# Key sums of two softmaxes, added over partitions by transfers and VectorE in place of products with ones

## The chip, the cores and the metric

One core of a Trainium2 chip runs the whole kernel. The metric is device time in microseconds, the median of several executions of the same program; lower is better.

## The reference

The input is a batch of 8 images of 512 channels and 32x32 pixels, so 8 elements of 512 channels by 1024 tokens. Two attention layers run one after the other, all in float32. The first has a layer norm, 8 heads of 64 channels and a residual; the second has a group norm, one head of 512 channels and a residual. Cut to what matters here:

```python
# layer 0: 8 heads
scores = jnp.einsum('bqhd,bkhd->bhqk', q, k) * scale
attn = jax.nn.softmax(scores, axis=-1)
out = jnp.einsum('bhqk,bkhd->bqhd', attn, v).reshape(B, S, C)
# layer 1: one head over all channels
logits = jnp.einsum('bcn,bcm->bnm', q, k) * scale
attn = jax.nn.softmax(logits, axis=-1)
o = jnp.einsum('bnm,bcm->bcn', attn, v)
```

Each softmax needs, for every query, the sum of the exponentials over all 1024 keys. How that sum is finished is what changes.

## The kernel before

**Layout.** Scores are computed transposed: keys lie on the partitions (8 blocks of 128 keys), queries along the row. A tile of exponentials `p` is 128 keys by 1024 numbers. The sum over keys is therefore made in two parts: VectorE adds the 8 tiles `p` into one tile `sum` of 128x1024, and then the 128 partitions of that tile must be added up.

**Layer 0, by pairs.** A `Pair` is two heads with one half (512) of the queries, so an element has 8 pairs. `Pair.scores` does, for each of 8 key blocks, two matmuls (L683), one exp on ScalarE (L686) and one add on VectorE (L690, L692). `Pair.values` does 16 matmuls (L701) into a bank `acc`. The loop over pairs runs scores of pair i+1, then values of pair i. After the values of each even pair, `invert_pairs` finishes the sums of that pair and the next: four matmuls with a matrix of ones (L715), each into 32 partitions of a PSUM bank `den`, give the sums, copied over 32 partitions. Then VectorE transposes in blocks of 32 (`compact`, L491) so that 128x16 different numbers stand in one column of each block, takes reciprocals and notes a check (`invert_sums`, L657, L661); ScalarE copies rows of them to the partitions where they are used (`rr`, L728); VectorE spreads them again by transposing a broadcast (`expand`, L496). The even pair's output is copied out of `acc` by ScalarE unscaled (L705) and multiplied later (L736); the odd pair's is multiplied on the way out (L708).

**Layer 1, `Whole`.** Its products use a seven-step scheme (`STEPS`), each step a few matmuls, with copies by ScalarE (`u1`, `u2`, `u3`) and adds by VectorE (L343) between them. `key_sums` adds the exponentials into two tiles `total`, `inverse` finishes them with four matmuls (L830) and the same transposing, and `values` uses the result `rden` when a block of the output is done (L870). The product `vm` (`project_v`, two units of seven steps) lies between the scores and the values; before, `inverse` stands between its two units.

**Order.** TensorE, ScalarE, VectorE and GpSimd run their instructions in the order in which the program writes them. Small work is put into a queue `side` by `later`; `tick` takes one item from it after each key block of `values` and after each step of the seven-step products. A list `at_scores` holds work that is done after the fifth block (m = 4) of the next `scores`. Loads and stores go through SyncE's queue (SP). GpSimd's queue carries only `save_w` (L210) for the first element and then stands empty. SBUF is shared out in 46 `big` tiles of 128x1024 and 9 `half` tiles of 128x512; an instruction that writes a new tile waits until the former user of its place is done.

Of the kernel before, what the change touches and what calls it, by code (L numbers as in the profile page):

```python
# [11 lines left out]
F32 = mybir.dt.float32  # L12
I32 = mybir.dt.int32
AF = mybir.ActivationFunctionType
ALU = mybir.AluOpType
# [4 lines left out]
P = 128  # L20
# [46 lines left out]
def fast_path(ctx: ExitStack, tc: tile.TileContext, x: bass.AP, vecs: dict, weights: dict, out: bass.AP,  # L67
# [35 lines left out]
    def half_tile(name):  # L103
        return half.tile([P, HB], F32, tag="h", name=name)
# [4 lines left out]
    def bank(name):  # L109
        return ps_a.tile([P, HB], F32, tag="a", name=name)  # L110
# [201 lines left out]
    def later(*work):  # L312
        side.extend(work)
# [341 lines left out]
    def invert_sums(r, sums):  # L655

        nc.vector.reciprocal(r, sums)  # L657
        i = n_checks[0]
        n_checks[0] += 1
        rows = sums.shape[0]  # L660
        nc.vector.scalar_tensor_tensor(sums, sums, 1.0, r, ALU.mult, ALU.add, accum_out=checks[:rows, i : i + 1])  # L661


    class Pair:
# [29 lines left out]
                    while at_scores:  # L694
                        at_scores.pop()()

        def values(self):
            acc = bank(f"acc_{self.tag}")
            for m in range(NM):
                for i in range(2):  # L700
                    nc.tensor.matmul(acc[i * D : (i + 1) * D, :], value_of(self.vt, m, self.c * P + i * D, D),  # L701
                                     self.p[m][:, ts(i, HB)], start=(m == 0), stop=(m == NM - 1))
                tick()
            if self.c % 2 == 0:
                nc.scalar.copy(self.o, acc)  # L705
            else:
                until(lambda: self.rden is not None)
                nc.vector.tensor_mul(self.o, acc, self.rden)  # L708

    def invert_pairs(two):  # L710


        den = bank(f"den_{two[0].tag}")
        for k in range(4):
            nc.tensor.matmul(den[ts(k, BL), :], ones[:, :BL], two[k // 2].sum[:, ts(k % 2, HB)],  # L715
                             start=True, stop=True)
        t = half_tile(f"dent_{two[0].tag}")
        r = small.tile([P, HB // BL], F32, tag="r", name=f"r_{two[0].tag}")
        rr = [small.tile([P, HB // BL], F32, tag=f"rr{n}", name=f"rr_{pair.tag}") for n, pair in enumerate(two)]
        rden = [half_tile(f"rden_{pair.tag}") for pair in two]  # L720

        def invert():
            invert_sums(r, compact(t, den))

        def copies():
            for n in range(2):
                for j in range(4):
                    nc.scalar.copy(rr[n][ts(j, BL), :], r[ts(2 * n + j // 2, BL), :])  # L728

        def rows(n):  # L730
            expand(rden[n], rr[n])
            two[n].rden = rden[n]

        at_scores.append(invert)
        later(lambda: [at_scores.pop()() for _ in list(at_scores)], copies, lambda: rows(1), lambda: rows(0),
              lambda: nc.vector.tensor_mul(two[0].o, two[0].o, rden[0]))  # L736

    def project_out(b, w, ot, stats):

# [22 lines left out]
    class Whole:  # L762
# [50 lines left out]
        def operands(self, g):  # L813
# [7 lines left out]
            for n, l, r in (("T1", "12", "11"), ("T2", "22", "T1"), ("T3", "22", "12"), ("T4", "21", "T2")):  # L821
                later(lambda n=n, l=l, r=r: sub(n, l, r))

        def inverse(self):
            b = self.b
            den = bank(f"den1_{b}")
            for a in range(2):
                for hf in range(NH):
                    k = 2 * a + hf
                    nc.tensor.matmul(den[ts(k, BL), :], ones[:, :BL], self.total[hf][:, ts(a, HB)],  # L830
                                     start=True, stop=True)
            t = half_tile(f"den1t_{b}")
            both, r = (small.tile([P, HB // BL], F32, tag=n, name=f"{n}_{b}") for n in ("both", "r1"))
            rr = small.tile([P, NH, HB // BL], F32, tag="rr", name=f"rr1_{b}")

            def invert():
                d = compact(t, den)
                nc.vector.tensor_copy(both[:D, :], d[D:, :])
                nc.vector.tensor_add(both[:D, :], both[:D, :], d[:D, :])
                invert_sums(r[:D, :], both[:D, :])  # L840

            def copies():
                for j in range(4):
                    for hf in range(NH):
                        nc.scalar.copy(rr[ts(j, BL), hf, :], r[ts(hf, BL), :])  # L845

            def rows():
                self.rden = big_tile(f"rden1_{b}")
                expand(self.rden, rr.rearrange("p a k -> p (a k)"))

            later(nothing, invert, copies, rows)

        def values(self, v):
            b = self.b
# [44 lines left out]
    with tc.manual_schedule(engines=ORDERED):  # L899
# [67 lines left out]
        for b in range(B):  # L967
            more = b + 1 < B
            stats = small.tile([P, NC, NH, 6], F32, tag="stats", name=f"stats_{b}")
            ot = {"tag": f"o_{b}"}  # L970
            first = Pair(b, 0, 0, qt, kt, vts, ot)
            first.scores(range(NM))
            q_last.rest()
            pairs = [first] + [Pair(b, hf, c, qt, kt, vts, ot) for hf in range(NH) for c in range(NC) if hf + c > 0]
            for i, p in enumerate(pairs):
                if i + 1 < len(pairs):
                    pairs[i + 1].scores(range(NM))
                if i < 2 and more:
                    until(lambda: ln.done)
                    later(*(lambda j=j, a=a, i=i: ln.affine(j, i, a) for j in range(2) for a in range(2)))  # L980
                if i == 1 and more:
                    wk_next = load_w("k", b + 1)
                if i == 6:
                    wo_now = load_w("o", b)
                if i == 7 and more:
                    hb = operands(ln.result())
                    add_operands(hb)
                p.values()
                if i % 2 == 0:
                    invert_pairs(pairs[i : i + 2])  # L990
            if more:
                k_units, kn = project(f"k{b + 1}", wk_next, bias_of("bk0"), hb, True)
                k_units[0].rest()
            wa_now = load_w("a", b)
            ob = operands(ot)
            o_units, x1 = project_out(b, wo_now, ob, stats)
            o_units[0].step(1)
            add_operands(ob)
            o_units[0].step(1)
            o_units[1].step(2)  # L1000
            for u in o_units:
                u.rest()
            wm_now = load_w("m", b)

            def meanwhile(n):
                if more:
                    k_units[1].step((2, 1, 3, 1)[n])

            h1 = group_norm(b, x1, stats, meanwhile)
            x1_away = {ik: put_away(wide(t), f"x1_away_{b}_{ik[0]}{ik[1]}") for ik, t in x1.items()}  # L1010
            h1b = operands(h1)
            add_operands(h1b)
            a_units, qa = project(f"qa{b}", wa_now, lambda oc: ua[:, oc : oc + 1], h1b)
            a_units[0].step(2)
            meanwhile(3)
            if more:
                kn_away = {ik: put_away(wide(t), f"k_away_{b + 1}_{ik[0]}{ik[1]}") for ik, t in kn.items()}
            a_units[1].step(2)
            for u in a_units:
                u.rest()  # L1020
            whole = Whole(b, qa, h1b, x1_away)
            s_units = whole.scores()
            whole.query_sums()
            for u in s_units[:2]:
                u.step(2)
            for u in s_units[:2]:
                u.rest()
            whole.key_sums(0)
            whole.operands(0)
            for u in s_units[2:]:  # L1030
                u.rest()
            whole.key_sums(1)
            whole.operands(1)
            v_units, vm = project_v(f"vm{b}", wm_now, h1b)
            v_units[0].rest()
            until(lambda: whole.summed)
            whole.inverse()
            v_units[1].rest()
            if more:
                wv_next, wq_next = load_w("v", b + 1), load_w("q", b + 1)  # L1040
            o_units = whole.values(vm)
            check = iter(()) if more else all_checks()
            for u in o_units:
                u.step(2)
                next(check, None)
            for u in o_units:
                u.rest()
            until(lambda: not side)
            if more:
                kt = {ik: block(f"k{b + 1}_again_{ik[0]}{ik[1]}") for ik in kn_away}  # L1050
                for ik, d in kn_away.items():
                    nc.sync.dma_start(out=wide(kt[ik]), in_=d)
                ln, vts, qt, q_last = next_values_and_queries(b + 1, wv_next, wq_next)
# [384 lines left out]
```

## Time and profile before

| | |
|---|---|
| three runs | 2967.59, 2969.01, 2970.05 us; median 2969.01 |
| the profiled execution | span 2967.7 us, granted TensorE clock 0.998 |
| matmuls at L715 (32 groups of 8) | 34.1 us busy |
| matmuls at L830 (8 groups of 8) | mean 604 ns of one |
| DMA | 217.32 MB, mean 73 GB/s |

A group's busy time counts the time in which at least one of its matmuls runs, so groups whose matmuls overlap show less than count times mean. Each float32 matmul of the program shows as two in the profile. A row of the profile names line, engine, operation, the tile written and the tiles read, and what the engine had waited for. The whole table of groups is long; these are the ones of attention on VectorE and ScalarE:

```profile
L686 ACT ACTIVATE p<-s 128x1024 f32<-128x1024 f32 x512 | 476.1, 1051 | 173.4 <-PE s L683 173.4
L692 DVE TENSOR_TENSOR sum<-sum,p 128x1024 f32<-128x1024 f32 x384 | 470.4, 1225 | 38.9 <-DVE sum L692 0.9
...
L728 ACT COPY rr<-r 32x16 f32<-32x16 f32 x256 | 51.7, 202 | 32.4 <-DVE r L657 28.5
```

### The profile page before, as it was taken

What the parts mean: (1) busy time and instruction counts of PE and PEld (TensorE: products, weight loads), DVE (VectorE), ACT (ScalarE), POOL (GpSimd) and SP (SyncE); (2) the same over time, 40 slices, a digit from 0 to 9 for tenths busy, and PEclk for the clock granted to TensorE, in tenths of its full rate; (3) what the DMA queues carried; (4) which work ended last, traced back from release to release, by engine and by line L of the source; (5) the groups of instructions that cost most, each with busy time, mean ns of one, the idle gap of its engine ahead of it and who ended that gap; (6) DMA issues with size and microseconds to landing.
All of it is one profiled execution on the core that took longest, in us unless ns stands there. A gap on an engine that the chain in (4) does not pass through costs nothing.

```text
span 2967.7 us, 26543 instructions
## 1 busy us (share of the span) xinstructions
PE 2945.7 (99%) x10043; PEld 1378.4 (46%) x10043; DVE 1773.6 (60%) x2266; ACT 1030.9 (35%) x1617; POOL 22.1 (1%) x37
## 2 busy tenths in 40 slices
PE   8999999999999999999999999999999999999999
PEld 4534455345543455434553345533455334553344
DVE  6676456765476654765546655576555665536744
ACT  4462215612155131641216412263222632225230
POOL 2000000000000000000000000000000000000000
PEclk9999999999999999999999999999999999999999
DMA  8103130031301213012130122201231021300201
GB/s 304 44 25 128 46 124 25 32 129 40 124 25 54 106 54 110 25 59 101 54 110 25 61 99 67 97 25 61 100 101 63 25 93 67 106 29 33 99 4 55
DMA packets 84920, 217.32 MB, mean 73 GB/s; under 512 B 8704, under 2 KB 12848, under 8 KB 84784
## 3 DMA queue, kind: packets, MB, share of 16 engines
q1 hardware_dynamic: 81616, 204.51, 19.9%
q0 software_dynamic: 3072, 11.01, 1.0%
q8 instruction: 81, 1.33, 0.2%
q14 instruction: 55, 0.45, 0.0%
q10 hardware_dynamic: 96, 0.02, 0.0%
HBM read 156.26 MB, written 59.24 MB: 73 GB/s over the span
## 4 chain that ended last, share of the span: by engine, by line
PE 97%; DVE 1%; DMA 1%; issue 0%; ACT 0%; SPq 0%; DVEq 0%
PE s L683 15%; PE acc L701 15%; PE x_o L429 6%; PE x_s L421 6%; PE y_s L421 4%; PE y_o L429 4%; PE z_o L429 4%; PE z_s L421 4%; PE x_q L404 3%; PE x_k L404 3%; PE x_vm L413 3%; PE x_qa L404 3%; PE x_v L413 3%; PE x_out L404 2%; PE y_q L404 2%; PE z_qa L404 2%
## 5 line engine op out<-in xcount | busy, mean ns | idle before, releaser
L686 ACT ACTIVATE p<-s 128x1024 f32<-128x1024 f32 x512 | 476.1, 1051 | 173.4 <-PE s L683 173.4
L692 DVE TENSOR_TENSOR sum<-sum,p 128x1024 f32<-128x1024 f32 x384 | 470.4, 1225 | 38.9 <-DVE sum L692 0.9
L701 PE MATMUL acc<-p,v 128*64 128x512 f32 x2048 | 453.6, 595 | 0.0
L683 PE MATMUL s<-q,k_again 64*128 64x512 f32 x1792 | 399.8, 596 | 0.0
L701 PEld LDWEIGHTS acc<-p,v 128*64 128x64 f32 x2048 | 141.4, 137 | 305.0 <-issue 286.1
L683 PEld LDWEIGHTS s<-q,k_again 64*128 64x128 f32 x1792 | 166.6, 186 | 232.1 <-ACT p L686 103.9
L690 DVE TENSOR_TENSOR sum<-p,p 128x1024 f32<-128x1024 f32 x64 | 78.4, 1225 | 195.2 <-ACT p L686 195.2
L421 PE MATMUL x_s<-S_qa,T_gn 128*128 128x512 f32 x256 | 120.3, 592 | 0.0
L429 PE MATMUL x_o<-T_p,S_vm 128*128 128x512 f32 x256 | 115.2, 592 | 0.0
L791 ACT ACTIVATE p<-p 128x512 f32<-128x512 f32 x128 | 80.8, 631 | 73.0 <-DVE p L343 73.0
L343 DVE TENSOR_TENSOR p<-u(1, 1)_s,y_s 128x512 f32<-128x512 f32 x32 | 22.1, 689 | 132.3 <-ACT u(1, 1)_s L434 132.3
L451 ACT ACTIVATE u(0, 0)_k<-x_k,vecs 128x512 f32<-128x512 f32 x16 | 11.0, 687 | 247.9 <-PE x_k L404 247.9
L343 DVE TENSOR_TENSOR y<-u(1, 1)_o,y_o 128x512 f32<-128x512 f32 x16 | 11.0, 688 | 132.5 <-ACT u(1, 1)_o L434 132.5
L421 PEld LDWEIGHTS x_s<-S_qa,T_gn 128*128 128x128 f32 x256 | 48.6, 190 | 61.2 <-issue 61.2
L429 PEld LDWEIGHTS x_o<-T_p,S_vm 128*128 128x128 f32 x256 | 48.6, 190 | 60.7 <-issue 60.7
L705 ACT COPY o<-acc 128x512 f32<-128x512 f32 x32 | 18.8, 586 | 155.3 <-PE acc L701 155.3
L496 DVE STREAM_TRANSPOSE rden<-rr 128x512 f32<-128x512 f32 (+1 forms) x72 | 51.6, 750 | 26.4 <-ACT rr L845 13.6
L728 ACT COPY rr<-r 32x16 f32<-32x16 f32 x256 | 51.7, 202 | 32.4 <-DVE r L657 28.5
L413 PE MATMUL x_vm<-w_m,T_gn 128*128 128x256 f32 x256 | 60.5, 379 | 0.0
L343 DVE TENSOR_TENSOR qa<-u(1, 1)_qa,y_qa 128x512 f32<-128x512 f32 x16 | 11.0, 688 | 82.4 <-ACT u(1, 1)_qa L451 82.4
L421 PE MATMUL y_s<-S_qa,gn 128*128 128x512 f32 x128 | 60.2, 593 | 0.0
L421 PE MATMUL y_s<-S_qa,T_gn 128*128 128x512 f32 x128 | 60.1, 592 | 0.0
(321 smaller groups left out, 4440.7 us busy)
## 6 DMA issues: line engine op xcount, KB each, us to landing
x<-in_x_dram SPq DMA_DIRECT2D x32, 512.0 KB, 6.5
xr<-in_x_dram SPq DMA_DIRECT2D x64, 256.0 KB, 2.6
x_away<-x SPq DMA_DIRECT2D x32, 512.0 KB
x1r<-x_away SPq DMA_DIRECT2D x64, 256.0 KB, 5.1
out_dram<-y SPq DMA_DIRECT2D x64, 256.0 KB, 2.5
k_away<-k SPq DMA_DIRECT2D x28, 512.0 KB, 2.6
k_again<-k_away SPq DMA_DIRECT2D x28, 512.0 KB, 6.3
w_o<-saved_o SPq DMA_DIRECT2D x24, 512.0 KB, 4.6
```

The source lines that it names most:

```text
L404: nc.tensor.matmul(dst, a[:, k, ts(r, P)], b[:, k, :], start=(opens and k == 0), stop=(k == 1), skip_group_check=True)
L413: nc.tensor.matmul(dst[:, ts(m, CB)], b[:, k, ts(2 * r + m, P)], a[:, k, :], start=(opens and m == 0 and k == 0), stop=(k == 1), skip_grou ...
L421: nc.tensor.matmul(dst, b[:, k, ts(r, P)], a[:, k, :], start=(opens and k == 0), stop=(k == 1), skip_group_check=True)
L429: nc.tensor.matmul(dst, a[:, m, ts(r, P)], b[m // 2][:, m % 2, :], start=(opens and m == 0), stop=(m == NM // 2 - 1), skip_group_check=True)
L496: nc.vector.transpose(t.rearrange("p (k i) -> p k i", i=BL), r.unsqueeze(2).to_broadcast((P, r.shape[1], BL)))
L683: nc.tensor.matmul(s[:, ts(i, HB)], self.k[m // 4][r, ts(m % 4, P)], self.q[r, :], start=True, stop=True)
L686: nc.scalar.activation(p, s, AF.Exp, scale=1.0 / float(D) ** 0.5)
L690: nc.vector.tensor_add(self.sum, self.p[0], p)
L692: nc.vector.tensor_add(self.sum, self.sum, p)
L701: nc.tensor.matmul(acc[i * D : (i + 1) * D, :], value_of(self.vt, m, self.c * P + i * D, D), self.p[m][:, ts(i, HB)], start=(m == 0), stop ...
L728: nc.scalar.copy(rr[n][ts(j, BL), :], r[ts(2 * n + j // 2, BL), :])
L791: nc.scalar.activation(dest(i, k), dest(i, k), AF.Exp, scale=float(C) ** -0.5)
```

## The change

The partitions of the sums are added by transfers. `halve` adds the upper 64 partitions of a sum to the lower 64 with an accumulating DMA transfer issued from GpSimd. `fold` then brings each half row of 512 as 2x32 partitions into a 32-partition quarter of a half tile, the first 32 by a plain transfer and the second 32 by an accumulating one. VectorE transposes the folded tile in blocks of 32 and reduces each block's row of 32 (`folded_sums`), which gives the same 128x16 sums as `compact` did.

For the pairs, this is done for the first three groups of each element; the last group keeps the products with ones. In the folded groups the inversion moves one pair later (it is put into `at_scores` after the odd pair), both pairs' outputs are copied by ScalarE unscaled, and both are multiplied by VectorE later. For `Whole`, the four matmuls of `inverse` go; `fold` is put into `side` after the last key sums; and `inverse` moves from between the two `vm` units to after the first step of the first output unit, written directly and not through `side`.

The diff, cut:

```diff
--- before.py
+++ after.py
@@ -694,46 +694,77 @@
                     while at_scores:
                         at_scores.pop()()
-        def values(self):
+        def values(self, scaled):
             acc = bank(f"acc_{self.tag}")
             for m in range(NM):
                 for i in range(2):
                     nc.tensor.matmul(acc[i * D : (i + 1) * D, :], value_of(self.vt, m, self.c * P + i * D, D),
                                      self.p[m][:, ts(i, HB)], start=(m == 0), stop=(m == NM - 1))
                 tick()
-            if self.c % 2 == 0:
+            if not scaled:
                 nc.scalar.copy(self.o, acc)
             else:
                 until(lambda: self.rden is not None)
                 nc.vector.tensor_mul(self.o, acc, self.rden)
-    def invert_pairs(two):
-        den = bank(f"den_{two[0].tag}")
-        for k in range(4):
-            nc.tensor.matmul(den[ts(k, BL), :], ones[:, :BL], two[k // 2].sum[:, ts(k % 2, HB)],
-                             start=True, stop=True)
-        t = half_tile(f"dent_{two[0].tag}")
-        r = small.tile([P, HB // BL], F32, tag="r", name=f"r_{two[0].tag}")
-        rr = [small.tile([P, HB // BL], F32, tag=f"rr{n}", name=f"rr_{pair.tag}") for n, pair in enumerate(two)]
-        rden = [half_tile(f"rden_{pair.tag}") for pair in two]
-        def invert():
-            invert_sums(r, compact(t, den))
-        def copies():
+    def fold(f, q, t, cols):
+        for n in range(2):
+            nc.gpsimd.dma_start(out=f[ts(q, BL), :], in_=t[ts(n, BL), cols], accum_op=ALU.add if n else ALU.bypass)
+    def halve(t):
+        nc.gpsimd.dma_start(out=t[:D, :], in_=t[D:, :], accum_op=ALU.add)
+    def folded_sums(d, t, f):
+        nc.vector.transpose(t, f)
+        nc.vector.tensor_reduce(d, t.rearrange("p (k i) -> p k i", i=BL), mybir.AxisListType.X, ALU.add)
+    class PairSums:
+        def __init__(self, two):
+            self.two, self.tag = two, two[0].tag
+            self.r = small.tile([P, HB // BL], F32, tag="r", name=f"r_{self.tag}")
+            self.rr = [small.tile([P, HB // BL], F32, tag=f"rr{n}", name=f"rr_{p.tag}") for n, p in enumerate(two)]
+        def fold(self):
+            self.f = half_tile(f"fold_{self.tag}")
+            for pair in self.two:
+                halve(pair.sum)
+            for n, pair in enumerate(self.two):
+                for i in range(2):
+                    fold(self.f, 2 * n + i, pair.sum, ts(i, HB))
+        def invert_folded(self):
+            d = small.tile([P, HB // BL], F32, tag="d", name=f"d_{self.tag}")
+            folded_sums(d, half_tile(f"foldt_{self.tag}"), self.f)
+            invert_sums(self.r, d)
+        def product(self):
+            self.den = bank(f"den_{self.tag}")
+            for k in range(4):
+                nc.tensor.matmul(self.den[ts(k, BL), :], ones[:, :BL], self.two[k // 2].sum[:, ts(k % 2, HB)],
+                                 start=True, stop=True)
+        def invert(self):
+            invert_sums(self.r, compact(half_tile(f"dent_{self.tag}"), self.den))
+        def copies(self):
             for n in range(2):
                 for j in range(4):
-                    nc.scalar.copy(rr[n][ts(j, BL), :], r[ts(2 * n + j // 2, BL), :])
-        def rows(n):
-            expand(rden[n], rr[n])
-            two[n].rden = rden[n]
-        at_scores.append(invert)
-        later(lambda: [at_scores.pop()() for _ in list(at_scores)], copies, lambda: rows(1), lambda: rows(0),
-              lambda: nc.vector.tensor_mul(two[0].o, two[0].o, rden[0]))
+                    nc.scalar.copy(self.rr[n][ts(j, BL), :], self.r[ts(2 * n + j // 2, BL), :])
+        def rows(self, n):
+            pair = self.two[n]
+            pair.rden = half_tile(f"rden_{pair.tag}")
+            expand(pair.rden, self.rr[n])
+        def scale(self, n):
+            pair = self.two[n]
+            nc.vector.tensor_mul(pair.o, pair.o, pair.rden)
     def project_out(b, w, ot, stats):
@@ -821,20 +852,22 @@
             for n, l, r in (("T1", "12", "11"), ("T2", "22", "T1"), ("T3", "22", "12"), ("T4", "21", "T2")):
                 later(lambda n=n, l=l, r=r: sub(n, l, r))
+        def fold(self):
+            self.f = half_tile(f"fold1_{self.b}")
+            for hf in range(NH):
+                halve(self.total[hf])
+            for a in range(2):
+                for hf in range(NH):
+                    fold(self.f, 2 * a + hf, self.total[hf], ts(a, HB))
         def inverse(self):
             b = self.b
-            den = bank(f"den1_{b}")
-            for a in range(2):
-                for hf in range(NH):
-                    k = 2 * a + hf
-                    nc.tensor.matmul(den[ts(k, BL), :], ones[:, :BL], self.total[hf][:, ts(a, HB)],
-                                     start=True, stop=True)
-            t = half_tile(f"den1t_{b}")
             both, r = (small.tile([P, HB // BL], F32, tag=n, name=f"{n}_{b}") for n in ("both", "r1"))
             rr = small.tile([P, NH, HB // BL], F32, tag="rr", name=f"rr1_{b}")
             def invert():
-                d = compact(t, den)
+                d = small.tile([P, HB // BL], F32, tag="d", name=f"d1_{b}")
+                folded_sums(d, half_tile(f"fold1t_{b}"), self.f)
                 nc.vector.tensor_copy(both[:D, :], d[D:, :])
                 nc.vector.tensor_add(both[:D, :], both[:D, :], d[:D, :])
                 invert_sums(r[:D, :], both[:D, :])
@@ -848,7 +881,9 @@
                 self.rden = big_tile(f"rden1_{b}")
                 expand(self.rden, rr.rearrange("p a k -> p (a k)"))
-            later(nothing, invert, copies, rows)
+            invert()
+            copies()
+            rows()
         def values(self, v):
             b = self.b
@@ -985,9 +1020,19 @@
                 if i == 7 and more:
                     hb = operands(ln.result())
                     add_operands(hb)
-                p.values()
+                p.values(scaled=(p is pairs[-1]))
                 if i % 2 == 0:
-                    invert_pairs(pairs[i : i + 2])
+                    sums = PairSums(pairs[i : i + 2])
+                    if i + 2 < len(pairs):
+                        sums.fold()
+                    else:
+                        sums.product()
+                        later(sums.invert, sums.copies, lambda: sums.rows(1), lambda: sums.rows(0),
+                              lambda: sums.scale(0))
+                elif i + 1 < len(pairs):
+                    at_scores.append(sums.invert_folded)
+                    later(sums.copies, *(lambda s=sums, f=f, n=n: f(s, n) for f in (PairSums.rows, PairSums.scale)
+                                         for n in range(2)))
             if more:
                 k_units, kn = project(f"k{b + 1}", wk_next, bias_of("bk0"), hb, True)
                 k_units[0].rest()
@@ -1030,19 +1075,21 @@
             for u in s_units[2:]:
                 u.rest()
             whole.key_sums(1)
+            later(whole.fold)
             whole.operands(1)
             v_units, vm = project_v(f"vm{b}", wm_now, h1b)
-            v_units[0].rest()
-            until(lambda: whole.summed)
-            whole.inverse()
-            v_units[1].rest()
+            for u in v_units:
+                u.rest()
             if more:
                 wv_next, wq_next = load_w("v", b + 1), load_w("q", b + 1)
             o_units = whole.values(vm)
             check = iter(()) if more else all_checks()
-            for u in o_units:
-                u.step(2)
-                next(check, None)
+            o_units[0].step(1)
+            whole.inverse()
+            o_units[0].step(1)
+            next(check, None)
+            o_units[1].step(2)
+            next(check, None)
             for u in o_units:
                 u.rest()
             until(lambda: not side)
```

## The prediction

> **What bounds the kernel now.** I read the page's busy table first, then the chain that ended last.
>
> ```profile
> span 2967.7 us, 26543 instructions
> PE 2945.7 (99%) x10043; PEld 1378.4 (46%) x10043; DVE 1773.6 (60%) x2266; ACT 1030.9 (35%) x1617; POOL 22.1 (1%) x37
> ...
> PE 97%; DVE 1%; DMA 1%; issue 0%; ACT 0%; SPq 0%; DVEq 0%
> ```
>
> TensorE is busy for 2945.7 of 2967.7 us and is 97% of the chain. An instruction taken off TensorE therefore shortens the run by its own length, as long as nothing it was covering comes up in its place. VectorE (DVE) and ScalarE (ACT) have room, and GpSimd (POOL) is nearly empty. How much room, stretch by stretch, comes from the table of stages, cut at two pair lengths of element 3:
>
> ```profile
> 1244.00:1258.00 14.00, 14.00 (x66) 5.15 (x64) 11.92 (x16) 11.14 (x20) 0.00 (x0) 1.00 0.01 2
> 1258.00:1273.00 15.00, 15.00 (x74) 5.31 (x72) 8.50 (x8) 8.63 (x12) 0.00 (x0) 1.00 0.00 0
> ```
>
> The columns after the stretch and its length are PE, PEld, DVE, ACT and POOL busy time. DVE has 11.9 of 14 us in the fuller stretch and 8.5 of 15 in the other.
>
> Then the products that go away. In the chain in order of time, around one group of pairs and around the whole attention's product:
>
> ```profile
> 1229.74 6.44 PE acc L701 x30
> 1236.18 1.00 PE den L715 x8
> 1237.18 7.07 PE s L683 x32
> 1244.24 7.02 PE acc L701 x32
> ```
>
> ```profile
> 1463.87 1.73 PE y_vm L413 x8
> 1465.60 0.99 PE den L830 x8
> 1466.59 1.93 PE x_vm L413 x8
> 1468.52 1.73 PE z_vm L413 x8
> ```
>
> Columns: start, length, engine, tile, line, count. Four column sums of 128x512 show as eight matmuls. They run side by side and take 1.00 us, and the scores after them take the 7.07 us that they take everywhere. The product at L830 costs more than its 0.99: the step after it takes 1.93 instead of 1.73.
>
> **The Trainium skill.** "TensorEngine Tiling (Array Packing)", Tiling Modes, says that a change of tiling mode drains TensorE and that tiles of one mode run in parallel. The trace agrees with both: eight matmuls of mean 605 ns fit in 1.00 us, and the 0.20 us after L830 looks like a drain. "DMA: Bandwidth & Descriptors", Anatomy of one DMA, puts a transfer issued from GpSimd at 2.0 us plus bytes over 436e3 per us, mostly a wait for the write's receipt. That gives 3.2 us for 512 KB, and the quickest ones here landed in 3.1:
>
> ```profile
> saved_v<-w_v_first POOLq DMA_DIRECT2D x3, 512.0 KB, 3.1
> saved_m<-w_m_first POOLq DMA_DIRECT2D x3, 512.0 KB, 7.2
> ```
>
> The same page, Rules for kernel authors, says that an accumulate reads its destination and writes it later, and that whatever depends on it must wait for its semaphore. No accumulating transfer is in this trace. "SBUF - State Buffer", A bandwidth-pool intuition that's wrong, warns that some VectorE copies keep GpSimd from writing descriptors. The work beside the folds is two-input adds, which that page says are not of this kind, and POOL issued in 0.53 us beside such adds at L217.
>
> **The change, part by part.**
>
> *Removed from TensorE.* Each of 8 elements loses three of its four groups at L715 and its one at L830. 24 x 0.995 = 23.9 us, taking the start-to-next-start distance, which is the same in every group. For L830 the two steps around it should have taken 2 x 1.725 = 3.45; from 1463.87 to 1468.52 they took 4.65, so 1.20 each, and 8 x 1.20 = 9.6 us. Together 33.5 us, all on the path.
>
> *Added transfers.* Per element 4 folds of 10 transfers (2 halvings of 256 KB, 8 moves of 64 KB), 320 in all, on POOL's queue. The issue costs
>
> ```profile
> L210 POOL DMA_DIRECT2D saved_v<-w_v_first x4 | 2.1, 536 | 16.8 <-DVE w_v_first L217 16.7
> ```
>
> so 0.54 us each. Nothing else is on POOL after the first element's saves at 72 us, so what matters is the length of one chain. After the last sum: the second halving is issued (0.54); the first quarter's move lands (L); then the add into that quarter and the next quarter's move go out together and the latter lands (0.54 + L), three times; then the last add (L). That is 5L + 2.2 us. L for 64 KB by the page's price is 2.15 as an estimate. The add into a quarter also reads its destination, for which there is no row: it can't be quicker than a plain move, and it could be as slow as the crowded 7.2 us above. I take L = 2.5, so 14.7 us. If the framework orders moves into different partitions of one tile, the chain is eight landings, about 21 us.
>
> *When it must be done: pairs.* Element 3:
>
> ```profile
> 1226.50 7.87 DVE L692 TENSOR_TENSOR sum<-sum,p 128x1024 f32<-128x1024 f32 x6
> ...
> 1255.73 7.87 DVE L692 TENSOR_TENSOR sum<-sum,p 128x1024 f32<-128x1024 f32 x6
> ```
>
> The second pair's sum ends at 1234.4. The new invert_folded stands two scores later than that pair's, after the fourth of eight adds, at about 1255.73 + 3.9 = 1259.6, less the 1 us of den: 24 us later. Behind it on DVE stand three adds, and on ACT the rr copies, 1.7 us, then the next scores' exps. TensorE would feel it only when these exps are late, about 5 us further on: 29 us. 14.7 fits, and so does 21.
>
> *When it must be done: whole attention.*
>
> ```profile
> 1457.68 2.48 DVE L806 TENSOR_TENSOR sum<-sum,p 128x1024 f32<-128x1024 f32 x2
> ...
> 1479.52 1.22 DVE L228 TENSOR_TENSOR S_vm<-vm,vm 128x1024 f32<-128x1024 f32 x1
> ```
>
> The total is done at 1460.2; the inverse comes after the first S_vm, at about 1481 in new time: 21 us, 14.7 fits. If it is late, DVE stands with out(0,0) and the rest of S_vm behind it, and ACT with the rr copies and then u2. TensorE runs on until its fifth step of 3.43 us needs u2, at 1491.5. Counting back u2 (0.6), rr (1.7) and the DVE part (2.5) gives 1486.7, so 26.5 us are bearable.
>
> *SP.* The queue's own waits show the load of w_q standing behind L830:
>
> ```profile
> SPq L204 <- PE den L715: 112.1, 8, 16.0
> ```
>
> with the matmuls of both lines under one name. A tile that held a total is freed at 1466 now, and at about 1475 after. Behind that load is x1r, needed at 1487.3 and landing in 5.1, so nothing comes of it. xr uses tiles of the same pool as fold's, but later than the last fold.
>
> *DVE and ACT.* Each fold adds a reduction of 128x512. "VectorE: DVE Perf Modes", The perf-mode tier table, gives tensor_reduce the slowest rate only; the 512-wide adds here take 0.69. The transpose stays at 0.7. Three odd pairs per element go out as an ACT copy (0.59) and a DVE product (0.69) in place of one DVE product (0.69). So 4 x 0.69 = 2.8 us DVE and 1.8 us ACT per element, in stretches with 2 us or more free in every 14: nothing. The moved queue items are five per group as before.
>
> Sum: 2967.7 - 33.5 = 2934.2 us of span. The runs (2967.6 to 2970.1, median 2969.0) lie about 1.3 above the span, so 2935.5.
>
> **Rivals.** *One: a part is given back.* Sums stay in the big pool some 15 us longer, and an exp or a load could get such a tile's place; or one chain per element meets the load of w_k or w_o and is late by a little. The profile shows no wait of an exp on anything but scores, and DMA at 0.00 to 0.01 in the two stretches, which speaks against. At 1 to 3 us per element it gives back 8 to 24: 2944 to 2960.
>
> *Two: the time was not TensorE's.* If the den products only filled a time in which exps catch up, the wait comes back in full: about 2969. Against it: PEld waits for p are 0.6 us at most, and scores take 7.07 us whether den or values stand before them.
>
> *Three, the other side: slow accumulation.* If L grows, the chain outlasts both deadlines. Pairs lose 5L + 2.2 - 29, three times; whole attention loses 5L + 2.2 - 26.5. At L = 5.5 these are 0.7 x 3 + 3.2 = 5.3 us per element, 42 in all, so the break-even is near 5.4. At L = 6, 3.2 x 3 + 5.7 = 15.3, times 8 is 122: 3058. For it: 7.2 us is in the trace for crowded stores, and no accumulate is. Against it: that was four 512 KB stores in a row to DRAM; these are 64 KB, in SBUF, one or two at a time.
>
> **Chances.** All hidden, 2933 to 2940: 0.60. Rival one 0.14, two 0.06, three 0.20. 0.2% is 6 us, about what a measurement of this kernel tells from no change. Faster by more is the forecast and rival one, 0.74; within it rival two, 0.06; slower rival three, 0.20. The range leaves rival three out: 2932 to 2969, the low end for a switch that costs a little more than shown.
>
> **What would show it.** Right: no L830, 64 matmuls at L715, phases of 7.07 and 7.02 meeting without a gap, inversions that start without a wait. Wrong: DVE waiting on a DMA before the transposes, ACT's rr copies and then PEld waiting behind it; or landings above 5 us on POOL's queue.

## The result and the profile after

The changed kernel takes 2936.6 us (median of 4 runs, 2936.0 to 2937.4) against 2969.5 of the kernel before: a ratio of 0.989, 95% interval 0.9873 to 0.9907. The forecast was 2935.5.

The head of the page of the changed kernel, with the chain's shares by engine:

```profile
span 2935.6 us, 26956 instructions
PE 2914.7 (99%) x9787; PEld 1374.3 (47%) x9787; DVE 1788.5 (61%) x2298; ACT 1044.1 (36%) x1641; POOL 238.5 (8%) x357
...
PE 98%; DVE 1%; DMA 0%; issue 0%; ACT 0%; SPq 0%; DVEq 0%
```

TensorE has 31.0 us less to do, and stays as full as it was. Its chain in order of time shows the two seams in which a product with ones stood, around a folded group of pairs and between the two `vm` units:

```profile
1218.04 7.02 PE acc L701 x32
1225.06 7.07 PE s L683 x32
1232.13 7.02 PE acc L701 x32
```

```profile
1449.23 1.73 PE y_vm L413 x8
1450.96 1.73 PE x_vm L413 x8
```

Values and scores meet with nothing between them, and the 1.93 us step is back at 1.73. I compared every stretch of TensorE, from its start to the next stretch's start, between the two traces. The 24 seams after values lost 23.9 us together, the 8 seams of `vm` 9.55 us, 1.2 each. Of everything else in the loop only the z steps of the output product differ by more than 1 us in their sum (1.2 us less). The rest of the difference to the 32.1 us of the spans lies outside the loop: the first element's preparation is 1.5 us longer in this execution, and the tail after the last matmul 0.7 us.

What came in its place, on GpSimd's queue for the first group of element 3 (start, length, idle time before and what ended it):

```profile
1223.80 0.80 POOL L716 DMA_DIRECT2D sum<-sum  x1 [17.85 <-DVE sum L692]
1224.43 0.70 POOL L713 DMA_DIRECT2D fold<-sum  x1
1227.81 1.29 POOL L713 DMA_DIRECT2D fold<-sum  x2 [2.68 <-DMA fold<-sum]
1230.97 1.27 POOL L713 DMA_DIRECT2D fold<-sum  x2 [1.87 <-DMA fold<-sum]
1234.69 1.27 POOL L713 DMA_DIRECT2D fold<-sum  x2 [2.45 <-DMA fold<-sum]
1237.69 0.76 POOL L713 DMA_DIRECT2D fold<-sum  x1 [1.72 <-DMA fold<-sum]
```

This is the chain of five landings: the issues come in pairs, each pair waiting for a transfer. From the sum's end at 1223.2 to the last landing at 1240.0 it is 16.7 us. The table of transfers, with the last column in us from issue to landing:

```profile
sum<-sum POOLq DMA_DIRECT2D x64, 256.0 KB, 3.5
fold<-sum POOLq DMA_DIRECT2D x256, 64.0 KB, 2.4
```

And VectorE, in the same group and in the whole attention of the same element:

```profile
1243.61 3.88 DVE L692 TENSOR_TENSOR sum<-sum,p 128x1024 f32<-128x1024 f32 x3
1247.41 0.70 DVE L720 STREAM_TRANSPOSE foldt<-fold 128x512 f32<-128x512 f32 x1
1248.15 0.69 DVE L721 TENSOR_REDUCE d<-foldt 128x16 f32<-128x512 f32 x1
...
1463.69 1.22 DVE L228 TENSOR_TENSOR S_vm<-vm,vm 128x1024 f32<-128x1024 f32 x1
1464.82 0.70 DVE L720 STREAM_TRANSPOSE fold1t<-fold 128x512 f32<-128x512 f32 x1
```

Neither transpose has an idle time before it in brackets, nor has any of the other 30: VectorE never waits for a fold here. The reduction takes the 0.69 us that the prediction gave it.

The room is not the same everywhere. The third group of the last element is the tightest: its chain shares the DMA engines with the load of w_o, its first move holds up the next pair of issues for 7.7 us, and the chain takes 21.2 us. It landed at 2733.3, 1.2 us before VectorE came to it:

```profile
2712.60 0.81 POOL L716 DMA_DIRECT2D sum<-sum  x1 [13.05 <-DMA w_o<-saved_o]
2713.17 0.77 POOL L713 DMA_DIRECT2D fold<-sum  x1
2720.86 1.28 POOL L713 DMA_DIRECT2D fold<-sum  x2 [6.92 <-DMA fold<-sum]
```

```profile
2734.43 0.70 DVE L720 STREAM_TRANSPOSE foldt<-fold 128x512 f32<-128x512 f32 x1
```

### The profile page after: what moved, and what is told of

It reads as the page before. It is cut to its first block, busy times and chain, and to the rows that moved or that the text cites. A ratio compares the mean times of both kernels' runs of the same rounds, so it can differ in the third digit from the quotient of the medians.

```text
span 2935.6 us, 26956 instructions
## 1 busy us (share of the span) xinstructions
PE 2914.7 (99%) x9787; PEld 1374.3 (47%) x9787; DVE 1788.5 (61%) x2298; ACT 1044.1 (36%) x1641; POOL 238.5 (8%) x357
## 4 chain that ended last, share of the span: by engine, by line
PE 98%; DVE 1%; DMA 0%; issue 0%; ACT 0%; SPq 0%; DVEq 0%
PE s L683 15%; PE acc L701 15%; PE x_o L429 6%; PE x_s L421 6%; PE y_s L421 4%; PE y_o L429 4%; PE z_s L421 4%; PE z_o L429 4%; PE x_q L404 3%; PE x_k L404 3%; PE x_qa L404 3%; PE x_v L413 3%; PE x_vm L413 3%; PE x_out L404 3%; PE y_q L404 2%; PE z_qa L404 2%
## 5 line engine op out<-in xcount | busy, mean ns | idle before, releaser
L716 POOL DMA_DIRECT2D sum<-sum x64 | 54.9, 859 | 2294.9 <-PE z_vm L413 1139.3
L713 POOL DMA_DIRECT2D fold<-sum x256 | 171.2, 764 | 292.5 <-DMA fold<-sum 281.6
L705 ACT COPY o<-acc 128x512 f32<-128x512 f32 x56 | 32.8, 586 | 197.4 <-PE acc L701 197.4
L343 DVE TENSOR_TENSOR p<-u(1, 1)_s,y_s 128x512 f32<-128x512 f32 x32 | 22.0, 689 | 132.3 <-ACT u(1, 1)_s L434 132.3
L343 DVE TENSOR_TENSOR y<-u(1, 1)_o,y_o 128x512 f32<-128x512 f32 x16 | 11.0, 688 | 134.7 <-ACT u(1, 1)_o L434 134.7
L343 DVE TENSOR_TENSOR qa<-u(1, 1)_qa,y_qa 128x512 f32<-128x512 f32 x16 | 11.0, 687 | 82.4 <-ACT u(1, 1)_qa L451 82.4
```

The lines of the kernel that those rows point to most:

```text
L713: nc.gpsimd.dma_start(out=f[ts(q, BL), :], in_=t[ts(n, BL), cols], accum_op=ALU.add if n else ALU.bypass)
L716: nc.gpsimd.dma_start(out=t[:D, :], in_=t[D:, :], accum_op=ALU.add)
```

## The experiments

The theory is that TensorE's time leaves with its instructions, and that a fold costs nothing until it is later than some deadline. The rivals are those of the prediction: a part is given back, the time wasn't TensorE's, or slow transfers pass the deadline.

**One part at a time.** The first kernel is the changed one with the `Whole` of before:

```diff
-            later(whole.fold)
...
-            o_units[0].step(1)
-            whole.inverse()
+            v_units[0].rest()
+            until(lambda: whole.summed)
+            whole.inverse()
```

> Only the three groups of pairs per element are folded; the whole attention keeps its products with ones and its old place for the inverse. Theory (time leaves with the TensorE instructions, 24 groups of 0.995 us): 23.9 us off the kernel before, about 2945.6. Rival (a part is given back in new waits of the pairs, which the whole attention's saving covers up): less than 18 us off, above 2951.

Measured: 2946.7 us, ratio 0.9924 (0.9908 to 0.9941), 23 us below the kernel before. The seams after values lost 23.9 us, and those of `vm` nothing.

The second is the kernel before with only the whole attention's fold and its moved inverse, and the pairs as they were.

```diff
 +            later(whole.fold)
...
-            v_units[0].rest()
-            until(lambda: whole.summed)
-            whole.inverse()
-            v_units[1].rest()
+            for u in v_units:
+                u.rest()
...
-            for u in o_units:
-                u.step(2)
-                next(check, None)
+            o_units[0].step(1)
+            whole.inverse()
+            o_units[0].step(1)
```

> Only the whole attention's sums are folded and its inverse moved; the pairs keep their products. Theory: 8 times 1.20 = 9.6 us off the kernel before, about 2959.9. Rival (only the 0.99 us of the product goes, the 0.2 us beside it belongs to something else): 8.0 us off, about 2961.5; the profile's stretches around the place tell the two apart.

Measured: 2961.4 us, ratio 0.9972 (0.9961 to 0.9983), 8.3 us below. The time alone can't tell 9.6 from 8.0, the stretches can: each of the 8 seams of `vm` lost 1.18 to 1.20 us, 9.5 together, so the 0.2 us around the product did belong to it. The two parts add up; neither covers the other.

**What a group of products is made of.**

```diff
-        for k in range(4):
+        for k in (*range(4), *range(4)):
             nc.tensor.matmul(den[ts(k, BL), :], ones[:, :BL], ...
```

> The kernel before, with the four products with ones of each group of pairs issued twice (same result written twice). If a group's 1.0 us is mostly streaming of its eight matmuls, 32 groups cost 0.86 us more each: 27 us, about 2996. If it is mostly the switch of tiling mode, which both copies share, under 10 us more: below 2979.

Measured: 2998.2 us in one run. Each of the 32 seams grew by 0.85 to 0.87 us, 27.5 together. So 0.86 of the 1.0 us is what eight such matmuls cost behind others of their kind, and some 0.14 us is left for what surrounds the group.

**What accumulating costs.** All accumulates are turned into plain moves, so three quarters of the partitions are left out of the sums:

```diff
-... accum_op=ALU.add if n else ALU.bypass)
+... accum_op=ALU.bypass)
```

> All accumulating transfers are made plain ones, so that the additions over partitions are left out (each quarter holds one 32-partition part of the sums) and everything else stays. If accumulating costs a transfer much more than moving, landings of 64 KB and 256 KB fall clearly below the 2.4 and 3.5 us of the changed kernel and the chain of ten gets shorter; if not, they stay within 0.3 us. The total stays at 2936 within 2 us either way, since the chain is hidden.

Measured: 2934.4 us in one run, 2.2 below the changed kernel's median; the stretches show no more than 0.1 us difference at any of the folded seams, and nearly all of what TensorE gained lies in the first element's preparation and in one qa product of the last element. The table of transfers and GpSimd's queue of this run:

```profile
sum<-sum POOLq DMA_DIRECT2D x64, 256.0 KB, 2.9
fold<-sum POOLq DMA_DIRECT2D x256, 64.0 KB, 1.9
```

```profile
1225.81 0.99 POOL L713 DMA_DIRECT2D fold<-sum  x2 [2.30 <-DMA fold<-sum]
1228.49 0.99 POOL L713 DMA_DIRECT2D fold<-sum  x2 [1.69 <-DMA fold<-sum]
```

Landings fall from 2.4 to 1.9 and from 3.5 to 2.9 us: outside the 0.3 us that I had allowed for "no cost", but far from the 5.4 us of the slow rival. A step of the chain takes 2.7 us in place of 3.2, and an issue 0.50 us of GpSimd in place of 0.76. The difference is not the accumulates' alone: in the changed kernel the moves issued right behind an accumulate also land in 2.4 us (median) and take 0.77 us to issue.

**How late a fold may be.** Three kernels repeat one plain move in the chain, each repeat waiting for the one before; nothing is left out of the computation. The first has three repeats in each chain of pairs and two in each of the whole attention, the second five in the whole attention's alone, the third seven in those of the pairs alone.

```diff
-    def fold(f, q, t, cols):
-        for n in range(2):
+    def fold(f, q, t, cols, pad=0):
+        for n in (*[0] * pad, 0, 1):
```

> The changed kernel with its chains made longer by repeats of one plain move that each wait for the one before: 3 repeats in each chain of pairs, 2 in each of the whole attention, some 2.7 us each (from the steps of the run with plain transfers). Chains of about 24.4 and 22.8 us from the last sum. Theory (TensorE feels a late fold only from 27 to 29 us in the pairs and from 26.5 us in the whole attention): no change, 2937 within 3 us, although VectorE waits some 3.5 us in each whole attention. Rival (TensorE loses what VectorE waits): 8 times 3.5 = 28 us more, about 2965.

> As before it, with 5 repeats in the whole attention's chain only: about 30.9 us. Theory: 4.4 us past the 26.5, 8 times, 35 us more: about 2972, with the waits of TensorE before the fifth step of the output's first unit. Rival (the inverse isn't near TensorE's path): 2937.

> As before it, with 7 repeats in the chains of pairs only: about 35.2 us. Theory with the deadline of the prediction, 29 us: 6.2 us times 24 = 149, about 3085. With 27 us, which the changed kernel's trace suggests (the copies rr must end 0.6 us before the exp that the third scores bank waits for): 8.2 times 24 = 197, about 3134. Rival (deadlines don't bind, VectorE catches up): 2937.

Measured, one run each: 3028.4, 3018.7 and 3222.4 us. A repeat took some 2.1 us and not 2.7, and yet all three lost far more than the theory gave them: 92, 82 and 286 us over the changed kernel. No rival gave as much either. The deadlines were wrong, and the traces show which.

*Seven repeats, pairs.* First group of element 3, VectorE and then TensorE:

```profile
1349.14 3.88 DVE L692 TENSOR_TENSOR sum<-sum,p 128x1024 f32<-128x1024 f32 x3
1360.80 0.71 DVE L720 STREAM_TRANSPOSE foldt<-fold 128x512 f32<-128x512 f32 x1 [7.78 <-DMA fold<-sum]
```

```profile
1358.69 2.85 PE L683 MATMUL s<-q,k_again 64*128 64x512 f32 x12
1365.85 6.26 PE L683 MATMUL s<-q,k_again 64*128 64x512 f32 x20 [4.32 <-ACT p L686]
```

VectorE waits 7.8 us, TensorE 4.3 us, on the exps behind the `rr` copies. So about 3.5 us of VectorE's wait are hidden. In the changed kernel VectorE comes to this fold 24.2 us after the sum, so 27.6 would be free; here the fold came 32.0 us after it. That is near the 27 us read off the changed kernel's trace. In the second group VectorE comes 22.4 us after the sum and 3.4 us of its wait are hidden: 25.8.

*The third group* is another matter. In the run with three repeats the first two groups cost 1.1 us in all, and nearly the whole loss of the pairs is at the last product: the stretch from values(6) to the k product grew by 7.5 to 11.1 us in every element. VectorE and then TensorE there:

```profile
1335.07 3.89 DVE L692 TENSOR_TENSOR sum<-sum,p 128x1024 f32<-128x1024 f32 x3
1345.09 0.71 DVE L720 STREAM_TRANSPOSE foldt<-fold 128x512 f32<-128x512 f32 x1 [6.13 <-DMA fold<-sum]
...
1346.94 3.88 DVE L692 TENSOR_TENSOR sum<-sum,p 128x1024 f32<-128x1024 f32 x3
```

```profile
1350.88 1.92 PE L749 MATMUL den<-sum,ones 128*32 128x512 f32 x4 [5.15 <-DVE sum L692]
```

The three adds behind the inversion finish the sum of pair 7, and that is what the last group's product on TensorE reads; it follows values(6) with no time between. Here all but 1.0 us of VectorE's wait reaches TensorE (6.13 and 5.15). VectorE comes to this fold 22.4 us after the sum, so the deadline is 23.4 us. This chain was also longer than its repeats make it. The load of w_o ran beside it, though no run takes that load away:

```profile
1321.45 1.29 POOL L713 DMA_DIRECT2D fold<-sum  x2 [2.67 <-DMA fold<-sum]
1326.58 1.28 POOL L713 DMA_DIRECT2D fold<-sum  x2 [3.84 <-DMA fold<-sum]
1329.80 0.52 POOL L713 DMA_DIRECT2D fold<-sum  x1 [1.94 <-DMA fold<-sum]
1335.33 0.50 POOL L713 DMA_DIRECT2D fold<-sum  x1 [5.00 <-DMA fold<-sum]
```

Two steps of 5.1 and 5.5 us stand where 3.2 and 2.1 are usual.

*Whole attention, five repeats.* TensorE and the stages around its wait (PE, PEld, DVE, ACT and POOL busy, then the granted clock):

```profile
1510.58 6.11 PE L429 MATMUL z_o<-p,vm 128*128 128x512 f32 x8 [8.01 <-DVE y L343]
1516.53 3.60 PE L429 MATMUL x_o<-T_p,S_vm 128*128 128x512 f32 x8
```

```profile
1502.50:1510.50 8.00, 0.07 (x1) 0.00 (x0) 5.08 (x10) 2.20 (x9) 0.00 (x0) 0.67 0.06 8
1510.50:1516.60 6.10, 6.02 (x9) 2.64 (x10) 3.74 (x5) 0.00 (x0) 0.00 (x0) 0.59 0.64 183
1516.60:1520.00 3.40, 3.40 (x10) 1.49 (x9) 2.13 (x3) 0.00 (x0) 0.00 (x0) 1.00 0.98 396
```

TensorE waits for `y` at L343, out(0,0) of the first unit, and it waits at its fourth step, the second unit's z. That product writes into the tile of which out(0,0) reads the other half. TensorE loses 8.0 us by waiting and another 2.5 because the next product runs at a granted clock of 0.59. VectorE waited 9.56 us before its transpose in this element, so 1.55 us of its wait were hidden, and the seven others show the same. In the changed kernel it comes to this transpose 19.3 us after the total, so a fold may land 20.9 us after it, and not 26.5. With two repeats, in the first of the three runs, the chains took 21.3 to 24.5 us and the whole attention lost 16.5 us in the eight elements.

What the three runs show of the deadlines, in us after the last sum:

| fold | VectorE comes to it | hidden of its wait | deadline | prediction | chain in the changed kernel |
|---|---|---|---|---|---|
| pairs, first group | 24.2 | 3.5 | 27.6 | 29 | 16.1 to 17.4 |
| pairs, second group | 22.4 | 3.4 | 25.8 | 29 | 16.2 to 16.4 |
| pairs, third group | 22.4 | 1.0 | 23.4 | 29 | 17.2 to 21.2 |
| whole attention | 19.3 | 1.55 | 20.9 | 26.5 | 17.0 to 17.4 |

**Folding the fourth group too.** The last group of each element that has a next one can be folded beside the k product. Its fold has to be quicker, so the first pair's transfers go ahead and the two quarters' moves go out together:

```diff
+            for n, pair in enumerate(self.two):
+                halve(pair.sum)
+                for part in range(2):
+                    for i in range(2):
+                        fold(self.f, 2 * n + i, pair.sum, ts(i, HB), part)
...
-                k_units[0].rest()
+                k_units[0].step(3)
+                sums.invert_folded()
+                sums.copies()
+                k_units[0].step(1)
+                for n in range(2):
+                    sums.rows(n)
+                for n in range(2):
+                    sums.scale(n)
+                k_units[0].rest()
```

> The changed kernel, with the fourth group of pairs folded as well in the seven elements that have a next one, its inversion put between the steps of the next element's k product, and each fold ordered so that the first pair's transfers run before the second pair's sum is there and the two quarters' moves go out together (about 10 us after the last sum in place of 16). Theory: seven more groups of 0.995 us leave TensorE and nothing waits, 7.0 us below the changed kernel: about 2929.7, 0.9866 of the kernel before. Rival (the pairs' output is needed too soon by the next product, so that TensorE waits where den stood): 2937 or more, with waits of TensorE on VectorE before the third step of out.

> The changed kernel with only the order of the pairs' folds made shorter as in the run before, the last group left to the products. Theory: the chain was hidden at 16 us and is hidden at 10, so no change: 2936.6 within 2. Rival (the chains of 16 us cost something somewhere, or the gain of the run before is that of the order): up to 7 us less.

Measured: all groups 2965.3 us, ratio 0.9991 (0.9983 to 1.0); the shorter order alone 2936.1, 0.9889 (0.9874 to 0.9904), the changed kernel's time. So the chain's length alone is worth nothing while it is hidden. Folding the fourth group took 1.15 us from each of seven elements at the seam after values, and gave back 4.0 to 6.2 us in each k product. VectorE and TensorE there:

```profile
1336.89 0.71 DVE L720 STREAM_TRANSPOSE foldt<-fold 128x512 f32<-128x512 f32 x1 [3.37 <-DMA fold<-sum]
...
1342.24 0.68 DVE L343 TENSOR_TENSOR k<-u(1, 1)_k,y_k 128x512 f32<-128x512 f32 x1
```

```profile
1337.72 1.88 PE L404 MATMUL z_k<-T_h,w_k 128*128 128x512 f32 x4
1342.98 3.35 PE L404 MATMUL y_k<-x,w_k 128*128 128x512 f32 x4 [3.38 <-DVE k L343]
```

The read of y_k's bank, k(1,1), stood behind inversion, rows and scales, and ahead of them the fold was late, since its moves met the load of w_a: their step took 7.2 us. Here a wait of 3.4 us is followed by a product of 3.35 us in place of 1.88. In six of the seven elements, with waits of 3.2 to 4.2 us, a slower stretch follows the wait; in the seventh, after 3.8 us, the product kept its full speed.

> As the run with all groups folded, and the sums over channels of the next element's variance (one product with ones of 1.0 us, between two steps of the q product) folded too in seven elements: one halving, two moves, two accumulates, and ten queue items later the transpose and reduction. Theory: a product between two steps of 128x128 matmuls costs 1.2 us, so 7 times 1.2 = 8.4 us less than the run with all groups, about 2921, if the later scaling of x hides beside the first pairs. Rival (the scaling comes too late for the first exps or keeps VectorE from the q steps): no gain or a loss, 2930 or more.

This kernel folded the variance's product of the next element as well. `folded_root` transposes the fold, reduces it, multiplies by 1/C and goes on as `root` does.

```diff
         def variance(self):
+            if self.b:
+                self.f = half_tile(f"varf_{self.b}")
+                halve(self.total)
+                for part in range(2):
+                    for k in range(NH):
+                        fold(self.f, k, self.total, ts(k, HB), part)
+                return
...
-            yield from self.root()
+            if self.b:
+                for _ in range(10):
+                    yield
+            yield from (self.folded_root() if self.b else self.root())
```

Measured: 2991.1 us, ratio 1.0075 (1.0061 to 1.0089), slower. The q product lost its 1.3 us of seam, and the second part of q took 16.8 to 18.7 us in place of 12.3: in element 3 TensorE waited 3.4 us for q(1,1) on VectorE, which stood behind three scalings of x. It looks like the same fault in another place; no run put q(1,1) ahead to show it, and the trace is of the slowest of five executions (3001.0 us).

Two runs then tell the order from the late landing:

```diff
                 sums.invert_folded()
-                sums.copies()
-                k_units[0].step(1)
+                k_units[0].step(2)
+                sums.copies()
```

> As the run with all groups folded, but in the k product VectorE's out(1,1) and ScalarE's third copy are written ahead of the rr copies, rows and scaling, so that y_k's bank is read before these. Theory (the 5 us lost in k are the bank read by out(1,1) standing behind the rr copies, rows and scales): most of the loss of 8 times up to 5 us goes; 7 us of den are then gained, about 2931 to 2935. Rival (the late landing of the fold itself holds TensorE): above 2945.

```diff
-            wa_now = load_w("a", b)
             ob = operands(ot)
             o_units, x1 = project_out(b, wo_now, ob, stats)
...
             for u in o_units:
                 u.rest()
+            wa_now = load_w("a", b)
```

> As the run before, and the load of w_a issued after the out product, so that it doesn't share the DMA engines with the last fold, whose moves took 7 us where 2.4 is usual. Theory: the fold lands 4 us earlier, VectorE doesn't wait, 2929.7 (seven groups of 0.995 us below the changed kernel). Rival (the later load of w_a is late for the qa product or pushes the loads behind it): 2936 or more.

Measured: with the order alone 2928.2 us, ratio 0.9865 (0.9848 to 0.9881); with the later load too 2926.8, 0.9859 (0.9843 to 0.9875). The order was the cause: k lost 0.6 us in all seven elements together, in place of 35.5, although VectorE still waited 2.9 to 3.6 us for each of these folds. The later load takes even that away, and the fold lands in time:

```profile
1308.56 1.04 POOL L713 DMA_DIRECT2D fold<-sum  x2 [2.98 <-DMA sum<-sum]
1310.72 1.59 POOL L713 DMA_DIRECT2D fold<-sum  x2 [1.12 <-DMA fold<-sum]
```

The step that took 7.2 us, and still 6.9 with the order alone, takes 2.2. The two last kernels differ only in where that load is issued, so the other 4.7 us were the sharing of the DMA engines. This kernel is 9.9 us below the changed one; 8.0 of it are the seven seams at 1.15 us. The two last kernels can't be told apart by their times (2926.6 to 2930.2 and 2925.5 to 2927.8).

## Why the prediction was right, and where not

**The gain.** The sum of 33.5 us was right in both its terms: 23.9 and 9.6 were forecast, 23.9 and 9.55 are what the seams lost, together and each part alone. Taking the start-to-next-start distance and, at L830, the two steps around it was the right reading of the trace. That the saving comes through in full was shown, not only argued, by the all but unchanged stretches everywhere else in the loop.

**The landing.** L = 2.5 us was close to the measured median of 2.4. Plain moves among themselves landed in 1.9, where the prediction had 2.15 as an estimate. The halvings take 3.5 us with accumulation, 2.9 without. The chain came to some 16.7 us in the group shown and not 14.7: 0.55 us pass before the second halving is issued, the first move holds up the next issue for 3.4 us, since it lands only after 3.1, and the three steps after it take 3.0 to 3.7 us in place of 3.04. The framework orders only transfers on the same partitions: moves into the next quarter go out behind the add without a wait.

**The deadline of the pairs.** 29 us was a rough size; 27.6 us is what the first group showed. The 24 us at which VectorE comes to the fold were right for that group, the only one that the prediction read; it is 22.4 in the two others. And the step "behind it on DVE stand three adds" stopped short of asking who reads them. In the third group these adds finish the sum that the last product on TensorE waits for, so that group has 1.0 us beyond VectorE's own 22.4. "14.7 fits, and so does 21" came true, but a chain of 21.2 us in the last element was 2.2 us from costing something, and not 8.

**The deadline of the whole attention.** This step failed: "TensorE runs on until its fifth step of 3.43 us needs u2". The fourth step in the written order is the second unit's first z, and it has to wait for out(0,0), on VectorE, behind the inverse. 26.5 us should have been 20.9. The place of the inverse was off too: 1481 "in new time" still holds the 1.2 us that the product took, and without them it is the 19.3 us measured and not 21. With the chain at about 17 us the conclusion held with some 3.5 us to spare. Had the framework ordered the eight landings, the 21 us that the prediction called harmless would have stood at this deadline. So the time was forecast by the right gain, while that nothing was given back rested in part on luck: the chain was short enough for deadlines that came earlier than the prediction thought.

**The rivals.** Slow accumulation is excluded by landings of 2.4 and 3.5 us. Its break-even was set too high, since the price of lateness was too low: waits begin earlier in all four places, and most waits of TensorE of 3 us or more are followed by a slower product. A give-back and "the time was not TensorE's" are excluded by the seams. The load of w_o does meet the third group's chain, as the first rival feared, and is hidden there, in the last element by 2.2 us.

## What to carry to other kernels

Where one engine is the chain, read an instruction's price as the distance between the starts of its neighbours with and without it, and look at both neighbours. Work moved off that engine onto a long path of transfers is free only up to a deadline, and the deadline is found by following the waiting engine's queue, in the written order, to the next read of a bank that TensorE writes again or to the next operand that it loads. Do it for every place of a loop: here four folds had four deadlines. To fold one more sum, first write such reads ahead of the wait, then see what loads share the DMA engines with the transfers.

## What the runs showed of the hardware

After a wait of 8.0 us TensorE's granted clock was 0.59 for the next 6 us and a product of 3.60 us took 6.11; after one of 3.4 us it was 0.57 and a product of 1.88 us took 3.35. So a late operand cost 2.5 and 1.5 us more than the wait. That the clock falls to half after an idle window of some 3.4 us, and needs as long a busy one to come back, is what the Trainium skill says in "TensorE: Matmul & The Clock Gate" (Part 1: The HAM clock gate). The wait of 8.0 us agrees with it. Near 3.4 us the runs show no sharp edge: in the run with all groups folded a wait of 3.2 us was followed by a stretch at half clock and one of 3.8 us was not, and the waits of 1.1 to 1.7 us in the run with three and two repeats never were. The prediction had left this cost out.

Accumulating within SBUF: 64 KB landed in 2.4 us (median) in the changed kernel and 1.9 with plain transfers alone, 256 KB in 3.5 against 2.9. A plain move issued right behind an accumulate was as slow as the accumulate. Issued with no other just before or after it, in the run with seven repeats, a plain move of 64 KB landed in 1.85 us and an accumulate in 2.3. Beside a load that kept the DMA engines at 0.97 to 1.0 for most of that time, a step of two 64 KB moves took 7.2 us in place of 2.2.
